# Gated cross attention on one core: the next quad's scores behind the last attention block, two transposes issued earlier, one sum in another buffer

## The chip, the cores and the metric

The kernel runs on one core of one Trainium2 chip. The metric is the device time of one execution in microseconds (us). Lower is better. The five engines of a core have queues of their own and run in parallel: PE (matrix products), DVE and POOL (elementwise work), ACT (activations and copies), and SP, which issues most of the transfers. [...] In profile lines PEld is the loading of weights into the PE array.

## What is computed

Eight sequences of 1024 rows (x, width 1024) attend to eight short memories (64 rows, width 512). Everything is float32.

```python
memory_proj = jnp.einsum('bme,de->bmd', memory, W_mem)
scores = jnp.einsum('bnd,bmd->bnm', hidden_states, memory_proj) / jnp.sqrt(jnp.float32(D))
attn = jax.nn.softmax(scores, axis=-1)
memory_context = jnp.einsum('bnm,bmd->bnd', attn, memory_proj)
gate_input = jnp.concatenate([hidden_states, memory_context], axis=-1)
gate = jax.nn.sigmoid(jnp.einsum('bnf,df->bnd', gate_input, W_gate) + b_gate)
fused = hidden_states + gate * memory_context
return _rmsnorm(fused, norm_w)
```

The large product is x (8192 x 1024) times the upper half of W_gate (1024 x 1024). The lower half is applied to the memory once (`mg`), so that attention needs only two products with 64 memory rows each: one gives the context, one its share of the gate.

## The kernel before, in words

**Quads.** The 8192 rows are cut into 16 quads of 512 rows, q = 0 to 15, two to a sequence. A quad's x is transposed into four tiles, a11, a12, a21 and a22 (`A[q, r, half]`), by eight instructions `transpose_x` on DVE: two for each tile.

**Products and slots.** The product with W_gate is done in Strassen-Winograd form at two levels. One quad has seven outer products, in the order 1, 6, 7, 5, 4, 2, 3 (`ORDER`, L527), and each has seven inner products A, B, C, D, A', E, F: A' adds onto A. One inner product is one slot, so a quad has 49 (`SLOTS`), slot 0 being A of outer product 1. In a slot PE issues two matmuls in the source, which are four records in the profile. In what follows C(5) is inner product C of outer product 5. In the profile all elementwise sums come from line 95 and all matmuls from line 92, so instructions are told apart by the names of their tiles.

**The sums around them.** These come with each outer product:

- `outer_s` (DVE) forms left operands of whole products. Those of a quad are S1 and S2 (for products 5 and 6), S3 = a11 - a21, written over a21 (for product 7), and S4 = a12 - S2 (for product 3).
- `inner_s(q, o, part)` (POOL) forms the left operands s1 to s4 of the inner products of o: part 0 gives s1 and s2, part 1 gives s3 and s4. They are put on the list one outer product ahead, at its slots 1 and 5, and are shown as tile `l`. B reads s2, C reads s3, D reads s1, F reads s4.
- u2, u3 and u4 (DVE) take B, C and D out of PSUM, each on top of the one before; ACT copies A first.
- `pre` (POOL) adds u3, u3 and u4 into output tiles, `fin` (DVE) adds A, D, E and F.
- `norm`, `gated` (DVE), `sigmoid`, `square` (ACT) and `residual` (a transfer from POOL's queue that adds x) finish a quad's output, partly during the next quad.

**The order.** Every engine runs its instructions in the order of the program (`pin`). That order is written by hand: `at(slot, ...)` puts work ahead of the matmuls of a slot, `mid((q, o), ...)` puts it behind the attention products of outer product o of quad q and ahead of its `fin` sums. Inside a slot the order is that of registration.

**Attention.** The last four outer products (5, 4, 2, 3) each hold a block of 16 matmuls between A' and E, two at a time: each uses 64 of the 128 rows of the array (`64*128` in the profile). They accumulate into A, F, E and D as well as into two tiles `pc`. `scores(q)` (L295) is 32 records in the profile on all rows and 64 columns (`128*64`), again two at a time, and a copy to `sT` on ACT; it reads all four tiles of x of its quad, k = 0 to 3 from a11 and a21 and the rest from a12 and a22. It stands ahead of slot 7, so between outer products 1 and 6. `transpose_scores` follows at slot 9, the softmax at slots 10 and 13, `transpose_attn` (tile `pa`) at slot 18.

**PSUM.** Five banks rotate over the tiles A to F. F shares B's bank. The next outer product's A, B, C, D and E take the banks of this one's C, D, A, E and F.

**Ahead of the loop.** The memory is projected (`pm`), its projection is spread over four tiles m11 to m22 (`mpT`), and `mg` is made by seven products with sums of the lower weights (`mg_product`). Their order is 1, 6, 5, 2, 7, 4, 3, and `mp_step` makes three sums for them. The third, s3 = m11 - m21 on POOL (L463), is read by product 7, the fifth of the seven. It lies in the rotating buffers `l2`, of which there are two; later tenants of the same pair are c21 and, in turn, the operands of `inner_s`. POOL's queue behind s3 reads: four inner sums of weight block 7, one sum for `mg`, `inner_s(0, 1, ...)` for the first quad, and twelve inner sums of the weight blocks 5, 6 and 4.

Of the kernel before, what the change touches and what calls it, by code (L numbers as in the profile page):

```python
# [10 lines left out]
ALU = mybir.AluOpType  # L11
# [9 lines left out]
def tile_gated_cross_attention_rmsnorm(  # L21
# [42 lines left out]
    nc = tc.nc  # L64
# [18 lines left out]
    rot = ctx.enter_context(tc.tile_pool(name="rot", bufs=2))  # L83
    small = ctx.enter_context(tc.tile_pool(name="small", bufs=1))
# [9 lines left out]
    def tt(eng, o, a, b, op):  # L94
        pin(eng.tensor_tensor(o, a, b, op))  # L95
# [4 lines left out]
    def t4k(pool, shape, tag, name):  # L100
        return pool.tile(shape, F32, tag=tag, name=name)
# [33 lines left out]
    for k in range(KD):  # L135
        t = t4k(*((gpool, [P, D], "gate") if k < 7 else (apool, [P, D], "s4")), f"w2_{k}")
# [28 lines left out]
    def w1_place(o):  # L165

        if o in (5, 6, 4):
            outer_b[o] = const.tile([P, 4, H], F32, tag=f"t{o}", name=f"t{o}")
        inner_t[o] = const.tile([P, 3, 2, C], F32, tag=f"it{o}", name=f"it{o}")
# [237 lines left out]
    def mp_step(eng, tag, pool, a, b, op):  # L407
        t = t4k(pool, [P, KH, HM], tag, f"mp_{tag}")
        tt(eng, t, a, b, op)
        return t  # L410
# [49 lines left out]
    s2 = mp_step(nc.vector, "s2", apool, s1, m11, ALU.subtract)  # L460
    outer_sum(7, 3, 7)
    w1_place(7)
    s3 = mp_step(nc.gpsimd, "l2", rot, m11, m21, ALU.subtract)  # L463
    for n in range(4):
        inner_sum(nc.gpsimd, 7, n)
    c11 = mg_tile(rot, "u", "mg_c11")
# [53 lines left out]
    def at(slot, fn, *args):  # L520
        due.setdefault(slot, []).append(lambda: fn(*args))

    def mid(key, fn, *args):
        beside.setdefault(key, []).append(lambda: fn(*args))
# [5 lines left out]
    def plan(q):  # L530
        t0 = SLOTS * q
        nxt = q + 1 < NQ
        order = [o for o, _ in ORDER]
        for i, o in enumerate(order):
            for part, t in ((0, 1), (1, 5)):
                if i + 1 < len(order):
                    at(t0 + 7 * i + t, inner_s, q, order[i + 1], part)
                elif nxt:
                    at(t0 + 7 * i + t, inner_s, q + 1, order[0], part)
        at(t0 + 7, scores, q)  # L540
        at(t0 + 7, outer_s, q, 3)
        at(t0 + 7, outer_s, q, 4)
        at(t0 + 9, transpose_scores, q)
        at(t0 + 10, softmax_a, q)
        at(t0 + 13, softmax_b, q)
        at(t0 + 18, transpose_attn, q)
        at(t0 + 21, attn_difference, q)
        if not nxt:
            at(t0 + 5, load_last)
            return  # L550
        at(t0 + 2, load_xq, q + 1)
        for t in (2, 3):
            mid((q, 5), transpose_x, q + 1, t, 0)
            mid((q, 2), transpose_x, q + 1, t, 1)
        for i, t, half in ((36, 0, 0), (38, 1, 0), (43, 0, 1), (45, 1, 1)):
            at(t0 + i, transpose_x, q + 1, t, half)
        mid((q, 3), outer_s, q + 1, 1)
        mid((q, 3), outer_s, q + 1, 2)
        if (q + 1) % QPB == 0:
            at(t0 + 10, load_mp, (q + 1) // QPB)  # L560
            at(t0 + 49, load_mg, (q + 1) // QPB)
        if q % QPB == 0:
            at(t0 + 8, add_bias, q // QPB)
# [249 lines left out]
    for q in range(NQ):  # L813
        plan(q)
        for o, ext in ORDER:
            outer_product(q, o, ext)
# [29 lines left out]
```

## Time and profile before

| what | us |
|---|---|
| three runs | 982.54, 982.60, 982.59 |
| their median | 982.59 |
| the profiled execution's own time | 982.54 |
| its span, first to last instruction | 980.7 |
| one quad in the middle, A(1) to the next A(1) | 55.05 |
| first A(1) of the loop, after the start of the span | 83.98 |

The span is what the views divide up; 1.84 us of the execution's own time lie outside it. Of the span PE is busy for 98%, DVE for 84%, POOL for 74% and ACT for 33%. TensorE's granted clock is 0.996 on average. Quads 1 to 14 repeat each other: four of them, measured from A(1) to A(1), took 55.04, 55.05, 55.05 and 55.05 us. One slot without a wait takes 0.864 us.

A line of the timeline gives the start, the time taken, the engine, the source line, the operation, the tiles it writes and reads with their sizes, and in brackets how long the engine had been idle and for whom it waited. A matmul's line with "x4" covers the four records of a slot, and its end is modelled; starts are what to compare.

### The profile page before, as it was taken

How to read it: one execution, taken by the hardware profiler on the slowest of the kernel's cores; microseconds unless marked ns; L12 is line 12 of the kernel's file. 1: busy time of each engine (PE TensorE's matmuls, PEld its weight loads, DVE VectorE, ACT ScalarE, POOL GpSimd, SP SyncE). 2: the span in 40 equal slices, each digit the busy share in tenths (PEclk: the TensorE clock that was granted, in tenths of full speed). 3: DMA queues.
4: the chain of work that ended last, by engine and by line, in shares of the span. 5: the costliest groups of instructions: out<-in, count | busy, mean ns of one | idle time of the engine just before them, and what ended most of it. 6: DMA issues, size and time to landing. Idle time of an engine off the chain costs nothing.

```text
span 980.7 us, 14277 instructions
## 1 busy us (share of the span) xinstructions
PE 965.9 (98%) x4938; PEld 770.1 (79%) x4938; DVE 819.0 (84%) x1487; ACT 324.9 (33%) x602; POOL 730.5 (74%) x881
## 2 busy tenths in 40 slices
PE   9999999999999999999999999999999999999995
PEld 7546788888888888888887888888887888888873
DVE  3877788979797988979797988979797988979787
ACT  1100234152333334161433334151433334151434
POOL 3329977878787887878787877878787877878772
PEclk9999999999999999999999999999999999999998
DMA  9865264381918364382918374482918374482612
GB/s 374 258 157 141 35 110 117 91 200 55 192 65 156 113 137 112 97 194 58 189 65 160 109 139 110 100 190 62 185 65 163 111 139 104 106 185 66 170 65 86
DMA packets 71255, 128.32 MB, mean 131 GB/s; under 512 B 12432, under 2 KB 49296, under 8 KB 70928
## 3 DMA queue, kind: packets, MB, share of 16 engines
q1 hardware_dynamic: 61760, 93.34, 35.3%
q0 software_dynamic: 9280, 33.56, 18.5%
q8 instruction: 39, 0.64, 0.3%
q10 hardware_dynamic: 144, 0.52, 0.2%
q14 instruction: 32, 0.26, 0.1%
HBM read 87.56 MB, written 39.85 MB: 130 GB/s over the span
## 4 chain that ended last, share of the span: by engine, by line
PE 93%; POOL 3%; DVE 2%; issue 1%; ACT 0%; DVEq 0%; POOLq 0%; ACTq 0%
PE kA L92 19%; PE pc L92 12%; PE kE L92 11%; PE kF L92 10%; PE kD L92 10%; PE kC L92 9%; PE kB L92 9%; PE psT L92 6%; PE pg L92 4%; PE pm L92 3%; POOL it L95 1%; DVE gate L95 1%; POOL l L95 1%; POOL gate L95 1%; PE pz L92 0%
## 5 line engine op out<-in xcount | busy, mean ns | idle before, releaser
L95 POOL TENSOR_TENSOR gate<-gate,u 128x256 f32<-128x256 f32 x336 | 270.4, 835 | 115.8 <-DVE u L95 110.1
L582 ACT ACTIVATE gate<-gate 128x512 f32<-128x512 f32 x128 | 79.0, 629 | 400.3 <-DVE gate L95 400.3
L95 POOL TENSOR_TENSOR l<-a 128x256 f32<-128x256 f32 x128 | 128.4, 1003 | 74.1 <-DVE a L95 55.8
L248 DVE STREAM_TRANSPOSE a<-xq 128x512 f32<-128x512 f32 x128 | 138.1, 1101 | 4.0 <-DMA mgd<-mpq 4.0
L92 PE MATMUL pc<-mg,attnT 64*128 64x256 f32 x512 | 127.4, 389 | 0.0
L611 DVE SCALAR_TENSOR_TENSOR gate<-gate,ss,nw_sb 128x512 f32<-128x512 f32 x120 | 126.0, 1059 | 1.1
L92 PE MATMUL kB<-it,l 128*128 128x256 f32 x448 | 115.1, 379 | 0.0
L92 PE MATMUL kD<-it,l 128*128 128x256 f32 x448 | 115.0, 379 | 0.0
L92 PEld LDWEIGHTS pc<-mg,attnT 64*128 64x128 f32 x512 | 90.6, 186 | 29.7 <-issue 21.2
L92 PE MATMUL kA<-w,a 128*128 128x256 f32 x384 | 98.7, 379 | 0.4 <-ACT u L726 0.4
L92 PEld LDWEIGHTS kB<-it,l 128*128 128x128 f32 x448 | 85.0, 190 | 11.9 <-DVE gate L95 0.4
L92 PEld LDWEIGHTS kD<-it,l 128*128 128x128 f32 x448 | 85.1, 190 | 11.6
L95 DVE TENSOR_TENSOR gate<-gate,pc 128x512 f32<-128x512 f32 x128 | 87.2, 681 | 5.8 <-ACT gate L582 5.8
L92 PEld LDWEIGHTS kA<-w,a 128*128 128x128 f32 x384 | 71.6, 190 | 10.2 <-ACT u L726 0.8
L95 POOL TENSOR_TENSOR l<-s 128x256 f32<-128x256 f32 x96 | 76.6, 797 | 1.6 <-PE kF L92 1.5
L726 ACT COPY u<-kA 128x256 f32<-128x256 f32 x112 | 40.5, 362 | 101.8 <-PE kA L92 99.7
L92 PE MATMUL kE<-it,a 128*128 128x256 f32 x256 | 69.0, 392 | 0.0
L95 DVE TENSOR_TENSOR u<-u,kB 128x256 f32<-128x256 f32 x112 | 45.5, 407 | 27.6 <-PE kB L92 24.9
L92 PE MATMUL kA<-t,s 128*128 128x256 f32 x256 | 67.4, 386 | 0.0
L92 PE MATMUL kC<-w,l 128*128 128x256 f32 x256 | 65.8, 379 | 1.4 <-POOL l L95 1.4
L92 PE MATMUL kF<-w,l 128*128 128x256 f32 x256 | 65.7, 379 | 0.0
L596 ACT ACTIVATE junk<-gate 128x1024 f32<-128x1024 f32 x60 | 63.5, 1058 | 1.9 <-DMA gate<-in_x 1.0
(123 smaller groups left out, 1996.4 us busy)
## 6 DMA issues: line engine op xcount, KB each, us to landing
xq<-in_x SPq DMA_DIRECT2D x64, 512.0 KB, 9.5
gate<-in_x POOLq DMA_DIRECT2D x60, 512.0 KB, 7.9
out<-gate SPq DMA_DIRECT2D x60, 512.0 KB, 2.6
w<-in_w_gate_t SPq DMA_DIRECT2D x8, 512.0 KB, 11.0
w<-in_w_gate_t SPq DMA_DIRECT2D x2, 2048.0 KB, 15.6
mg<-mgd SPq DMA_DIRECT2D x16, 256.0 KB, 3.8
mpd<-mpT SPq DMA_DIRECT2D x4, 512.0 KB, 3.7
mgd<-mpq SPq DMA_DIRECT2D x16, 128.0 KB, 2.7
```

The lines of the kernel that those rows point to most:

```text
L92: pin(nc.tensor.matmul(o, lhsT, rhs, start=start, stop=stop, skip_group_check=True))
L95: pin(eng.tensor_tensor(o, a, b, op))
L248: nc.vector.transpose(A[key][:, :, r * P : (r + 1) * P], chunks(xq[q][:, 4 * t : 4 * t + 4, :], KD)[:, half * KH : (half + 1) * KH],)
L582: pin(nc.scalar.activation(g, g, AF.Sigmoid))
L596: nc.scalar.activation(junk, O[q, t], AF.Square, accum_out=ss[:, t % 2 : t % 2 + 1])
L611: nc.vector.scalar_tensor_tensor(g[:, cols], g[:, cols], rstd[:, t % 2 : t % 2 + 1], nw_sb[:, cols], ALU.mult, ALU.mult,)
L726: pin(nc.scalar.copy(p1, kb["A"]))
```

## The change

The change has three edits.

1. `s3` of the memory's sums moves from the two rotating buffers `l2` to the single buffer `junk` of the pool `small`. Its earlier tenant is the block of zeros that warms up PE at the start; its next are the `square` results of quad 0, which come after its last outer product.
2. `scores(q)` stays ahead of slot 7 for quad 0 alone. The other quads' scores are issued one quad sooner, in `mid((q, 3), ...)`: right behind the attention products of outer product 3 of the quad before, ahead of E(3), and ahead of the two sums `outer_s(q + 1, 1)` and `(q + 1, 2)`.
3. The two transposes that finish a12 of the next quad move from slots 43 and 45 to slots 42 and 43, so that they are ahead of u2 and u3 of outer product 3.

```diff
@@ -460,7 +460,7 @@
     outer_sum(7, 3, 7)
     w1_place(7)
-    s3 = mp_step(nc.gpsimd, "l2", rot, m11, m21, ALU.subtract)
+    s3 = mp_step(nc.gpsimd, "junk", small, m11, m21, ALU.subtract)
     for n in range(4):
         inner_sum(nc.gpsimd, 7, n)
@@ -537,7 +537,8 @@
-        at(t0 + 7, scores, q)
+        if q == 0:
+            at(t0 + 7, scores, q)
         at(t0 + 7, outer_s, q, 3)
         at(t0 + 7, outer_s, q, 4)
@@ -552,8 +553,9 @@
-        for i, t, half in ((36, 0, 0), (38, 1, 0), (43, 0, 1), (45, 1, 1)):
+        for i, t, half in ((36, 0, 0), (38, 1, 0), (42, 0, 1), (43, 1, 1)):
             at(t0 + i, transpose_x, q + 1, t, half)
+        mid((q, 3), scores, q + 1)
         mid((q, 3), outer_s, q + 1, 1)
         mid((q, 3), outer_s, q + 1, 2)
```

## The prediction

> **What bounds the kernel now.** I read the granted clock first (0.996, nothing to explain there), then the busy times, then the waits of PE.
>
> ```profile
> PE 965.9 (98%) x4938; PEld 770.1 (79%) x4938; DVE 819.0 (84%) x1487; ACT 324.9 (33%) x602; POOL 730.5 (74%) x881
> ```
>
> ```profile
> POOL l L95 <- PE pg L92: 18.3, 1, 18.3
> ...
> PE kC L92 <- POOL l L95: 1.4, 1, 1.4
> ```
>
> The columns of a wait are the sum, how often, and the longest. PE is the bound, and hardly waits for an operand: once, 1.4 us, in the first quad, and three times, 1.6 us together, in the last. So time is won only by giving PE less to do or by removing that one wait, and is lost wherever PE is made to wait. The upper line is POOL's one long wait, ahead of the loop. The timeline of the first quad shows where it comes out:
>
> ```profile
> 100.09 1.03 PE L92 MATMUL kA<-w,a 128*128 128x256 f32 x4
> 101.11 1.13 PE L92 MATMUL kB<-it,l 128*128 128x256 f32 x4
> 103.60 1.13 PE L92 MATMUL kC<-w,l 128*128 128x256 f32 x4 [1.37 <-POOL l L95]
> 104.57 1.03 PE L92 MATMUL kD<-it,l 128*128 128x256 f32 x4
> ```
>
> A slot is 0.864 us, so D(7) was due at 100.09 + 3 x 0.864 = 102.68 and starts at 104.57: 1.89 us lost. POOL came late with s3 because its queue had stood still.
>
> Then the timeline of a quad in the middle, q = 8, with A(1) at 581.29, all engines, from F(1) to C(5):
>
> ```profile
> 586.47 1.03 PE L92 MATMUL kF<-w,l 128*128 128x256 f32 x4
> 587.43 3.67 PE L92 MATMUL psT<-a,mpb 128*64 128x256 f32 x32
> 587.53 0.42 DVE L95 TENSOR_TENSOR gate<-u,kF 128x256 f32<-128x256 f32 x1 [0.44 <-PE kF L92]
> 589.42 1.22 DVE L95 TENSOR_TENSOR a<-a,a 128x1024 f32<-128x1024 f32 x1 [1.47 <-PE psT L92]
> 590.57 1.22 DVE L95 TENSOR_TENSOR s<-a,s 128x1024 f32<-128x1024 f32 x1
> 590.73 1.64 POOL L95 TENSOR_TENSOR l<-a 128x256 f32<-128x256 f32 x1 [3.71 <-DVE a L95]
> 591.03 1.13 PE L92 MATMUL kA<-t,s 128*128 128x256 f32 x4
> 593.13 0.42 DVE L95 TENSOR_TENSOR u<-u,kB 128x256 f32<-128x256 f32 x1 [1.35 <-PE kB L92]
> ...
> 601.80 0.42 DVE L95 TENSOR_TENSOR u<-u,kC 128x256 f32<-128x256 f32 x1
> 602.36 2.10 POOL L95 TENSOR_TENSOR gate<-gate,u 128x256 f32<-128x256 f32 x3 [1.54 <-DVE u L95]
> 604.41 0.73 POOL L95 TENSOR_TENSOR l<-s 128x256 f32<-128x256 f32 x1
> 605.19 0.82 PEld L92 LDWEIGHTS kC<-t,l 128*128 128x128 f32 x4
> 605.39 0.81 PE L92 MATMUL kC<-t,l 128*128 128x256 f32 x3
> ```
>
> The reader is to see two things. During the scores (3.6 us) DVE and POOL catch up: DVE idles 1.47 and 1.35 us, POOL 3.71. From u2(6) at 593.13 to u3(7) at 601.80 no DVE line has an idle time in brackets. And at the end s3 for C(5) is ready at 604.41 + 0.73 = 605.14, with its weights loading from 605.19: the margin is about nothing. The scores at slot 7 are the breathing space that makes this chain just fit.
>
> **What the Trainium skill says.** "TensorEngine Tiling (Array Packing)", section Key Properties: changing the tiling mode, not just the tile, drains the array. The trace agrees: around the scores, 591.03 to 592.00 (B) and 586.47 to 587.43 are 0.97 and 0.96 where a slot is 0.864, and 587.43 to 591.03 is 3.60 for 16 pairs of 0.216 (3.456): 0.35 us for two switches. Around attention in outer product 5, A' at 607.12, E at 610.00, F at 610.97 give 3.85 less two slots and 8 pairs: 0.39. "SBUF — State Buffer", section Who interferes with whom: a DVE instruction with two SBUF inputs contends with a GpSimd instruction that reads SBUF. The trace agrees: POOL's s1 takes 1.64 beside S4, against a median of 0.73. "TensorE: Matmul & The Clock Gate", section Step-by-step: weights are loaded ahead of the running matmul. Here the load leads by 0.20; after a late operand that lead is gone (C and D of 103.60 and 104.57 are 0.97 apart, 0.10 extra).
>
> **Part 1, the switches.** Before, one quad has four switches for its scores and its last attention block, 0.35 + 0.39 = 0.74. After, the array goes from full to rows, rows to columns, columns to full: three. The direct switch between the two tilings isn't in this trace. Bounds: free (saves 0.37), or as dear as both it replaces (saves nothing). I take one average switch, 0.74 / 4 = 0.185, and so a saving of 0.185. It is on PE, which is the bound, in 15 quads: **-2.8 us** (0 to -5.5). The matmuls themselves and the ACT copy only move; no transfer moves with them. ACT waits over 7 us there for the next sigmoid, so the 0.37 us copy is hidden.
>
> **Part 2, what loses its cover.** All times here are us after A(1) of a quad. From B(6) on, PE runs earlier by 0.96 + 3.60 + 0.97 - 2 x 0.864 = 3.80. C(5), before at 24.10, would be due at 20.30.
>
> DVE: `fin` of F(1) starts at 6.24, as before, since F(1) does not move. Then S3 follows at once, with no scores to wait for; the wait that is late next is DVE's own queue. 0.34 to S3, 1.15 from S3 to S4, 1.15 from S4 to u2(6) (the same size of instruction), the packed 8.67 from u2(6) to u3(7), 0.42 for that: u3(7) is done at 17.97, before at 20.93. So DVE gains 2.96 where PE gains 3.80.
>
> POOL: the two sums for product 7 start with S3 and are done by about 10.7, so they don't matter. `pre` of product 7 waits for u3(7): 0.14 to start, 2.05 until s3 starts, 0.73 for s3, 0.05 to the load: 20.94. PE waits from 20.30 to 20.94 and loses 0.10 for the lead: 0.74. Smaller waits ahead of it are inside this one, not added: B(7) for the bank that `fin` of D(6) frees (0.1), `pa` for the softmax (0.2). Once PE has waited, the distances behind are again those of before, so it does not wait a second time in the quad; and since A(1) to F(1) of the next quad has slack (DVE idles 0.97 ahead of `fin` of E(1)), the same wait comes again in each of the quads 1 to 15.
>
> In the seven even quads from 2 on, POOL also has `add_bias` ahead of the `pre` of product 6 (0.83 us in quad 2, which was hidden in 1.7 us of waiting). Now it pushes s3(7) to about 14.4 to 14.8 where C(7) is due at 14.04: 0.5 to 0.95 with the lead, in place of 0.74. I take 0.85. Sum: 8 x 0.74 + 7 x 0.85 = **+11.9 us**. Bounds: 0.6 a quad if the lead costs nothing, 1.05 if a `norm` (0.75 alone, 1.05 beside POOL) is held up 0.3 by the second sum for product 7, which now falls on it: +9 to +15.8.
>
> **Part 3, the transposes.** Each takes 1.04 to the next start. u2 and u3 of product 3 move back by 1.04, u4 not. `gated` of product 2, between them, then ends at 632.42 instead of 631.38, and attention overwrites its tile at about 632.58: it just fits. 0, at most 0.1 a quad. POOL's `pre` of product 3 starts 1.04 later, hidden by the scores ahead of E(3).
>
> **Part 4, s3's buffer.** With it `inner_s(0, 1)` no longer waits for product 7 of `mg` at 70.4; next it waits for the transposes of a11, at 56.7, and the inner sums for DVE's `outer_sum` of 6 and 4 (62.0 and 68.9). POOL's list of twelve then ends near 78, not 91.2. In quad 2, whose POOL wasn't behind, s3(7) had 1.0 us to spare, and quad 0 keeps its scores at slot 7. So the 1.89 goes: **-1.9 us**. Against it: POOL now runs beside DVE's sums of b21 (64.2 to 66.7), which PE needs at 70.25; stretching them as other sums were stretched (0.69 to 1.4) uses 2.8 of these 3.6 us. Bounds -1.9 to -0.9.
>
> **The sum** against the execution's own 982.54 (span 980.7, 1.84 outside it; the median of the runs is 0.05 higher): 982.54 - 2.8 + 11.9 - 1.9 = 989.7.
>
> **The rivals.**
> - *No wait appears.* PE keeps its distance and the two gains stand: 982.54 - 2.8 - 1.9 = 977.8. For it: PE is the only bound on the page, and DVE and POOL idle 16% and 26%. Against it: that idle time isn't between F(1) and C(5). It decides from 0.31 us a quad (4.7 / 15): the chain from F(1) to s3(5) would have to be 0.43 shorter than summed. Chance 0.19.
> - *It balances:* about 0.3 us a quad, 982.5. Chance 0.06.
> - *POOL and DVE hold each other up:* the upper bound plus 0.1 a quad for `gated`: 982.54 + 17.3 - 2.8 - 1.9 = 995.1. For it, norms beside POOL took 1.05 to 1.24. Chance 0.13.
> - My forecast: 0.62. With its costs' bounds, its own range is 985 to 995.
>
> **Chances.** About 0.2% (2 us) can be told from no change. Slower 0.62 + 0.13 = 0.75, same 0.06, faster 0.19. The range goes from 979 to 996: below it lies the first rival but for its weaker forms (0.15 left out), above it the third's worst third (0.04).
>
> **What would show it.** Right: new waits of kC on POOL's `l` in product 5 (and in even quads in product 7), some 0.7 us each; a quad of about 55.6; DVE without idle time from `fin` of F(1) to u3(7); in quad 0 no wait at C(7). Wrong: quads of 54.9 without waits (then the chain was shorter), or a direct switch that costs more than 0.35.

## The result, and the profile after

| | before | after |
|---|---|---|
| median of four runs, us | 982.60 | 1022.66 |
| lowest and highest | 982.54, 982.68 | 1021.59, 1024.38 |
| the profiled execution's own time; its span | 982.54; 980.7 | 1021.59; 1019.8 |
| one odd quad in the middle, A(1) to A(1) | 55.05 | 55.64 |
| one even quad in the middle | 55.05 | 60.37 |
| mean granted clock | 0.996 | 0.986 |

The change makes the kernel slower by 4%: ratio 1.041, interval 1.0394 to 1.0425. The direction was forecast, the size was not: 989.7 was expected, and 33 us more came. The table already says where to look. Odd quads are what was predicted (55.6); the even ones, from quad 4 to quad 14, lose another 4.7 us each, and quad 2 another 3.0.

The page's first part and the list of waits of the kernel after (sum, how often, longest; PEld is the weight load, PE the product):

```profile
PE 979.6 (96%) x4938; PEld 775.8 (76%) x4938; DVE 843.5 (83%) x1487; ACT 327.2 (32%) x602; POOL 728.7 (71%) x881
```

```profile
PEld kB L92 <- DVE gate L95: 31.2, 15, 4.1
...
PEld kC L92 <- POOL l L95: 3.9, 8, 0.5
...
PE kB L92 <- DVE gate L95: 25.1, 7, 3.7
```

The busy shares hardly tell the two kernels apart: PE still shows 96%. The waits do. PE waits seven times, once per even quad from 2 on, for 25.1 us together. The eight waits of kC on POOL's `l` are the odd quads' and are the predicted ones. In the chain of work that ended last PE's share falls from 93% to 77%, and DVE has 13% of it.

**An odd quad.** Timeline of the kernel after, quad 9, whose A(1) is at 605.45, from `fin` of F(1) to D(5):

```profile
611.69 0.42 DVE L95 TENSOR_TENSOR gate<-u,kF 128x256 f32<-128x256 f32 x1 [0.44 <-PE kF L92]
612.03 1.22 DVE L95 TENSOR_TENSOR a<-a,a 128x1024 f32<-128x1024 f32 x1
613.16 1.22 DVE L95 TENSOR_TENSOR s<-a,s 128x1024 f32<-128x1024 f32 x1
614.30 0.41 DVE L95 TENSOR_TENSOR u<-u,kB 128x256 f32<-128x256 f32 x1
...
623.03 0.42 DVE L95 TENSOR_TENSOR u<-u,kC 128x256 f32<-128x256 f32 x1
623.59 2.10 POOL L95 TENSOR_TENSOR gate<-gate,u 128x256 f32<-128x256 f32 x3 [1.53 <-DVE u L95]
625.64 0.73 POOL L95 TENSOR_TENSOR l<-s 128x256 f32<-128x256 f32 x1
626.42 1.13 PE L92 MATMUL kC<-t,l 128*128 128x256 f32 x4
627.39 1.03 PE L92 MATMUL kD<-it,l 128*128 128x256 f32 x4
```

This is the predicted chain, link by link: F(1)'s sum, S3 at once, S4, u2(6) at 8.85 after A(1) (8.87 was summed), a packed DVE queue to u3(7), `pre`, s3, and C(5) at 20.97 (20.94). D follows C after 0.97, so the lead of the load is lost as expected.

**An even quad.** Quad 8, whose A(1) is at 545.08, from u3(6), which `pre` of product 6 reads, to B(7):

```profile
555.12 0.41 DVE L95 TENSOR_TENSOR u<-u,kC 128x256 f32<-128x256 f32 x1
...
555.73 0.83 POOL L372 DMA_DIRECT2D mg<-in_b_gate  x1
...
556.31 2.37 POOL L95 TENSOR_TENSOR gate<-gate,u 128x256 f32<-128x256 f32 x3
...
556.57 4.70 DVE L613 SCALAR_TENSOR_TENSOR gate<-gate,ss,nw_sb 128x512 f32<-128x512 f32 x1
...
558.37 0.99 POOL L95 TENSOR_TENSOR l<-a 128x256 f32<-128x256 f32 x1
...
559.05 0.98 POOL L95 TENSOR_TENSOR l<-a,l 128x256 f32<-128x256 f32 x1
559.73 0.97 POOL L95 TENSOR_TENSOR l<-s 128x256 f32<-128x256 f32 x1
560.78 1.07 POOL L95 TENSOR_TENSOR l<-l,s 128x256 f32<-128x256 f32 x1
...
561.52 0.41 DVE L95 TENSOR_TENSOR gate<-gate,kD 128x256 f32<-128x256 f32 x1
...
561.98 1.98 PE L92 MATMUL kB<-it,l 128*128 128x256 f32 x4 [3.57 <-DVE gate L95]
```

The reader is to see the norm at 556.57. It is one half of a `norm`, the same 128 x 512 instruction that takes 0.74 alone and 1.06 beside POOL. Here it takes 4.70. It stands ahead of the `fin` sums of product 6, and B(7) needs the bank that `fin` of D(6) frees: DVE is through with that at 561.93 and B(7) starts at 561.98. A(7) was at 557.38, so B(7) was due at 558.24 and is 3.74 late.

POOL meanwhile works off `add_bias` and seven sums with hardly a pause. They start 0.68 us apart (558.37, 559.05, 559.73), until s2 of product 5, which reads the s1 made just before it: 1.05 from 559.73 to 560.78 where the same pair takes 0.80 elsewhere. The norm ends in that step, at 561.27. All seven even quads show the same: one norm each of 4.68 to 4.81, and none over 1.6 elsewhere.

**The clock behind the wait.** The table by stage of the same quad (window, us, busy time and count of PE, PEld, DVE, ACT, POOL; then granted clock, DMA share, GB/s). The windows run from A(7) to B(7), B to C, C to D, and D to the transpose `pa` behind it:

```profile
557.38:561.98 4.60, 1.03 (x5) 0.57 (x4) 4.60 (x4) 1.27 (x2) 4.39 (x6) 1.00 0.63 124
561.98:563.75 1.77, 1.77 (x4) 1.42 (x5) 1.70 (x5) 1.72 (x5) 0.00 (x0) 0.54 0.73 296
563.75:565.46 1.71, 1.71 (x6) 1.35 (x4) 1.49 (x4) 1.26 (x2) 0.00 (x0) 0.50 0.00 0
565.46:566.36 0.90, 0.90 (x5) 0.75 (x4) 0.42 (x1) 0.00 (x0) 0.11 (x1) 0.97 0.65 264
```

After 3.57 us without a product PE is granted half its clock for two slots: 1.77 and 1.71 in place of 0.864, so 1.75 us more. That and the 3.74 make 5.49; the quad measures 60.37 against 54.87 (55.05 less the 0.185 of the switches), 5.50.

The slow clock does not follow every time. In quad 2 the same norm takes 4.68 and B(7) comes as late, 4.59 behind A(7), but the granted clock stays at 1.00 behind it and the next slots take 0.96 and 0.87. That quad takes 58.68. Against odd quads of 55.64 the seven even ones (58.68 and six of 60.36 to 60.49) lose 31.5 together in the profiled execution. So its 39 us (1021.59 less 982.54) divide, with the experiments' numbers below, into -1.6 for the buffer, +8.9 for the moved scores in fifteen quads, and +31.5 for the norm of the even quads: 38.8 by this sum. It is the fastest of the four executions; by the medians the difference is 40.1.

### The profile page after: what moved, and what is told of

Its sections match the earlier page's. It is cut to its first block, busy times and chain, and to the rows that moved or that the text cites. A ratio compares the mean times of both kernels' runs of the same rounds, so it can differ in the third digit from the quotient of the medians.

```text
span 1019.8 us, 14307 instructions
## 1 busy us (share of the span) xinstructions
PE 979.6 (96%) x4938; PEld 775.8 (76%) x4938; DVE 843.5 (83%) x1487; ACT 327.2 (32%) x602; POOL 728.7 (71%) x881
## 4 chain that ended last, share of the span: by engine, by line
PE 77%; DVE 13%; issue 6%; POOL 3%; DMA 1%; ACT 0%; DVEq 0%; POOLq 0%; ACTq 0%
PE kA L92 13%; PE pc L92 11%; PE kE L92 9%; PE kC L92 8%; PE kF L92 7%; PE kD L92 7%; PE kB L92 7%; PE psT L92 6%; PE pg L92 5%; DVE gate L95 3%; DVE gate L613 3%; PE pm L92 3%; DVE u L95 2%; POOL gate L95 2%; DVE a L95 2%
## 5 line engine op out<-in xcount | busy, mean ns | idle before, releaser
L95 POOL TENSOR_TENSOR gate<-gate,u 128x256 f32<-128x256 f32 x336 | 283.8, 886 | 139.6 <-DVE u L95 135.5
L92 PE MATMUL kB<-it,l 128*128 128x256 f32 x448 | 121.6, 396 | 25.2 <-DVE gate L95 25.1
L613 DVE SCALAR_TENSOR_TENSOR gate<-gate,ss,nw_sb 128x512 f32<-128x512 f32 x120 | 144.3, 1212 | 1.1
L95 POOL TENSOR_TENSOR l<-a 128x256 f32<-128x256 f32 x128 | 115.1, 899 | 39.3 <-PE kB L92 34.8
L95 DVE TENSOR_TENSOR gate<-gate,kE 128x256 f32<-128x256 f32 x112 | 45.5, 418 | 50.5 <-PE kE L92 45.6
L92 PE MATMUL kC<-w,l 128*128 128x256 f32 x256 | 70.9, 402 | 0.0
L95 DVE TENSOR_TENSOR gate<-gate,kF 128x256 f32<-128x256 f32 x112 | 45.6, 419 | 27.4 <-PE kF L92 23.0
```

The costliest lines, as they stand in the source:

```text
L92: pin(nc.tensor.matmul(o, lhsT, rhs, start=start, stop=stop, skip_group_check=True))
L613: nc.vector.scalar_tensor_tensor(g[:, cols], g[:, cols], rstd[:, t % 2 : t % 2 + 1], nw_sb[:, cols], ALU.mult, ALU.mult,)
```

## The experiments

### The buffer alone

The kernel before with edit 1 and nothing else. `e1_buffer_only`, as a diff to the kernel after:

```diff
-        if q == 0:
-            at(t0 + 7, scores, q)
+        at(t0 + 7, scores, q)
...
-        for i, t, half in ((36, 0, 0), (38, 1, 0), (42, 0, 1), (43, 1, 1)):
+        for i, t, half in ((36, 0, 0), (38, 1, 0), (43, 0, 1), (45, 1, 1)):
...
-        mid((q, 3), scores, q + 1)
```

> The kernel before with edit 1 alone (s3 in the other buffer). If the wait in quad 0 is worth what the changed kernel's trace shows there (1.89 us lost before, about 0.3 after), the time is 981.0 (980.7 to 981.3), with no waits of PE from quad 1 on. If the early inner sums cost DVE more than they free, it is 982.6 or above.

Measured: 980.74 against 982.35, ratio 0.9984 (0.9977 to 0.999), so -1.6 us. The timeline of quad 0, from C(7):

```profile
101.60 1.03 PE L92 MATMUL kC<-w,l 128*128 128x256 f32 x4
102.47 1.03 PE L92 MATMUL kD<-it,l 128*128 128x256 f32 x4
103.63 0.41 PE L342 MATMUL pa<-ident,e 128*128 128x128 f32 x2
103.87 1.03 PE L92 MATMUL kA<-w,a 128*128 128x256 f32 x4
```

C(7) follows B(7) without a wait. From D(7) to `pa` it is 1.16, though, 0.3 more than a slot: the softmax, until now hidden by the wait at C(7), is late next. That is the difference between the 1.9 predicted and the 1.6 found.

### Is it the moved scores, or `add_bias` with them?

What sets even quads apart is `add_bias`, a transfer from POOL's queue at slot 8, between the sums of product 6 and `pre`. `e2_bias_slot6` is the kernel after with that transfer two slots sooner, where POOL waits for S3 anyway:

```diff
         if q % QPB == 0:
-            at(t0 + 8, add_bias, q // QPB)
+            at(t0 + 6 if q else t0 + 8, add_bias, q // QPB)
```

> The changed kernel with add_bias at slot 6 in place of slot 8 (quads 2, 4, ... 14), so that POOL issues it while it waits for S3. Theory A (the 4.7 us norm comes from what add_bias does to POOL's queue directly ahead of pre of product 6): no norm over 1.3 us, all quads at about 55.6, 989.6 in total (988.5 to 991). Rival (the long norm belongs to even quads for another reason, such as the transfers of x, mg or out at that place): still 4.7 us and near 1022.

Measured: 989.68 against 982.35, ratio 1.0074 (1.0059 to 1.0089). Quads 1 to 14 take 55.58 to 55.65, no norm is over 1.32, and its waits are those of an odd quad, fifteen times:

```profile
PEld kC L92 <- POOL l L95: 7.3, 15, 0.5
PEld kB L92 <- DVE gate L95: 6.3, 15, 0.4
```

So one transfer, at this place, costs 33 us of the 40. Moving the scores costs 989.68 - 980.74 = 8.9 us over the buffer alone, 0.6 a quad, close to the predicted net of 0.74 lost and 0.185 gained.

Of the same two edits, the transposes are told apart by `f3_old_transposes`, which is `e2_bias_slot6` with edit 3 undone:

```diff
-        for i, t, half in ((36, 0, 0), (38, 1, 0), (42, 0, 1), (43, 1, 1)):
+        for i, t, half in ((36, 0, 0), (38, 1, 0), (43, 0, 1), (45, 1, 1)):
```

> The kernel with add_bias at slot 6 (989.7), but with the two transposes back at slots 43 and 45: edits 1 and 2 without edit 3. If edit 3 is worth nothing, as I costed it: 989.7 within 0.5. If the scores need it (they would wait for the last transpose), 0.5 us a quad or more: 997 or above.

Measured: 989.57, ratio 1.0072 (1.0057 to 1.0087), the same. Edit 3 is worth nothing that can be told here.

### What keeps the norm waiting?

In the kernel before the same transfer stood ahead of the same `pre`, with the same norm beside it, and nothing happened. Its timeline in quad 8:

```profile
538.07 0.83 POOL L372 DMA_DIRECT2D mg<-in_b_gate  x1
...
538.62 0.75 DVE L611 SCALAR_TENSOR_TENSOR gate<-gate,ss,nw_sb 128x512 f32<-128x512 f32 x1
...
539.29 0.42 DVE L95 TENSOR_TENSOR u<-u,kC 128x256 f32<-128x256 f32 x1
...
539.84 2.55 POOL L95 TENSOR_TENSOR gate<-gate,u 128x256 f32<-128x256 f32 x3 [0.95 <-issue]
...
540.74 1.06 DVE L611 SCALAR_TENSOR_TENSOR gate<-gate,ss,nw_sb 128x512 f32<-128x512 f32 x1
```

There POOL pauses 0.95 between the transfer and its sums. The profile names no releaser for it, but `pre` reads u3(6), which ends at 539.71, and `pre` starts 0.13 later. In quad 14, where the transfer is issued later, the releaser is named: 0.43 for DVE's `u`. After the change u3(6) ends at 555.53, before the transfer is issued at 555.73, so nothing is left to pause for: this is how moving the scores closed the gap. Two things are to be separated: the transfer, and the pause behind it.

The expectations below call "the shared port" the access to SBUF over which DVE and POOL would hold each other up, and "descriptor writing" what POOL would do to issue a transfer; both are suppositions there. The four kernels of this part add work and ran once each, so what is read from them is above all the norm in their traces.

**Something else in the transfer's place.** `e3_filler` is `e2_bias_slot6` with one more sum on POOL, over 208 columns, at the transfer's old place. It takes 0.62 us, as long as the load of the next kernel; `add_bias` takes 0.83. The sum stands in every quad from 1 on.

```diff
+    filler = t4k(small, [P, 208], "filler", "filler")
+
+    def fill():
+        tt(nc.gpsimd, filler, nw_sb[:, 0:208], nw_sb[:, 208:416], ALU.add)
...
+        if q:
+            at(t0 + 8, fill)
```

> As the kernel with add_bias at slot 6, and in each quad from 1 on a POOL sum of two slices of 208 columns into a spare tile at slot 8, where add_bias stood; it adds work and no transfer. Theory A1 (POOL, once late, runs from one ready instruction to the next, and the norm of DVE finds no gap at the shared port): long norms of 4 to 5 us in all 15 quads, some 60.4 us each, 1060 in total. Theory A2 (the descriptor writing of the transfer holds the port): no norm over 1.4 us; POOL is only 0.6 us later, 990 to 999.

Measured: 993.6, and no norm over 1.36. Its timeline shows the same position as in the kernel after, with the norm 0.24 to 0.26 behind the start of `pre` in both:

```profile
545.00 0.62 POOL L95 TENSOR_TENSOR filler<-nw_sb 128x208 f32<-128x208 f32 x1
...
545.58 2.55 POOL L95 TENSOR_TENSOR gate<-gate,u 128x256 f32<-128x256 f32 x3
545.82 1.04 DVE L620 SCALAR_TENSOR_TENSOR gate<-gate,ss,nw_sb 128x512 f32<-128x512 f32 x1
```

So theory A1 fails: a POOL queue that is merely full, or a norm that merely meets `pre` at this moment, is not the cause. It takes the transfer.

**Another transfer in its place.** `f2_plain_load` has, instead of that sum, a plain load from POOL's queue: 208 columns of norm_w, into a tile that nobody reads. `add_bias` stays at slot 6.

```diff
+    def fill():
+        pin(nc.gpsimd.dma_start(filler, norm_w[0:208].partition_broadcast(P)))
...
+        if q:
+            at(t0 + 8, fill)
```

> As the kernel with add_bias at slot 6, and in each quad from 1 on a plain load from POOL's queue (norm_w, 208 columns to 128 partitions of a spare tile, no accumulation) at slot 8; it adds work. Theory C1 (any transfer that POOL issues in that place does it): norms of 4 to 5 us in all 15 quads, 1055 to 1065. Theory C2 (it takes add_bias, its accumulation or its 256 KB): no norm over 1.6 us, 989 to 996.

Measured: 1073.58, above the range given, but with one norm of 4.46 to 4.48 in each of the fifteen quads, as theory C1 says. Quads 3 to 14 take 61.43 to 61.45, quads 1 and 2 take 60.15. The picture is that of the even quads:

```profile
580.83 0.62 POOL L239 DMA_DIRECT2D filler<-in_norm_w  x1
...
581.46 2.09 POOL L95 TENSOR_TENSOR gate<-gate,u 128x256 f32<-128x256 f32 x3
...
581.66 4.48 DVE L620 SCALAR_TENSOR_TENSOR gate<-gate,ss,nw_sb 128x512 f32<-128x512 f32 x1
...
586.85 2.08 PE L92 MATMUL kB<-it,l 128*128 128x256 f32 x4 [3.36 <-DVE gate L95]
```

So it does not take what `add_bias` does with its data: a small load does the same. The excess over the range is the clock. In most quads it stays low for longer than in the kernel after (three slots of 1.87, 1.71 and 1.70 in the quad shown; mean 0.952), though PE's wait is shorter (3.36); in quad 1 it is two slots, 1.84 and 1.68.

**A pause behind the transfer.** `f1_gap_after_bias` is the kernel after with four memsets on POOL behind `add_bias` in even quads. They only write. The sums follow 1.5 us later.

```diff
+    def fill():
+        for _ in range(4):
+            pin(nc.gpsimd.memset(filler, 0.0))
...
             at(t0 + 8, add_bias, q // QPB)
+            if q:
+                at(t0 + 8, fill)
```

> The changed kernel, add_bias at slot 8 as there, and directly behind it in the even quads four fills of a spare tile by POOL, which write SBUF and read nothing; they add work. Theory B1 (the norm is kept out by POOL's reading sums that follow the transfer without a gap): during the fills the norm gets through, no norm over 1.6 us, even quads within 1.5 us of 55.6, 989 to 1001 in total. Theory B2 (the transfer's descriptor writing alone keeps it out): norms of 4 to 5 us stay, 1020 or more.

Measured: 999.34, and no norm over 1.30:

```profile
546.89 0.83 POOL L378 DMA_DIRECT2D mg<-in_b_gate  x1
...
547.44 1.55 POOL L240 MEMSET filler<- 128x208 f32 x4
...
547.73 0.74 DVE L621 SCALAR_TENSOR_TENSOR gate<-gate,ss,nw_sb 128x512 f32<-128x512 f32 x1
...
548.96 2.54 POOL L95 TENSOR_TENSOR gate<-gate,u 128x256 f32<-128x256 f32 x3
```

Adding work to POOL took 23 us away, and theory B2 fails. The norm that began behind the transfer and beside writes alone ran at its own 0.74. What is left over `e2_bias_slot6`, 9.7 us, is POOL's delay: in even quads PE now waits 0.62 for B(7) and 0.91 for C(7).

**A dependent pair.** In the kernel after the norm ended where one POOL sum needed the result of the one just before. `g1_dependent_pair` puts such a pair directly behind `add_bias`: two sums that read, and no pause by idling or by writes.

```diff
+    def fill():
+        tt(nc.gpsimd, filler, nw_sb[:, 0:208], nw_sb[:, 208:416], ALU.add)
+        tt(nc.gpsimd, filler, filler, nw_sb[:, 208:416], ALU.add)
...
             at(t0 + 8, add_bias, q // QPB)
+            if q:
+                at(t0 + 8, fill)
```

> The changed kernel, add_bias at slot 8 as there, and directly behind it in the even quads two POOL sums of 208 columns, both reading SBUF, the second reading what the first wrote; they add work. In the traces the long norm ended where POOL came to such a pair (s2 on s1). Theory D1 (the wait of a dependent POOL sum on the one before is gap enough for the norm): no norm over 1.6 us, 994 to 1001. Theory D2 (it takes a longer stretch without reads, like the fills): norms of 4 us and more stay, 1022 or more.

Measured: 1001.67, 0.7 above the range given, and no norm over 1.33:

```profile
547.96 0.83 POOL L378 DMA_DIRECT2D mg<-in_b_gate  x1
...
548.53 0.91 POOL L95 TENSOR_TENSOR filler<-nw_sb 128x208 f32<-128x208 f32 x1
...
548.79 1.21 DVE L621 SCALAR_TENSOR_TENSOR gate<-gate,ss,nw_sb 128x512 f32<-128x512 f32 x1
...
549.52 0.96 POOL L95 TENSOR_TENSOR filler<-filler,nw_sb 128x208 f32<-128x208 f32 x1
```

From the first sum of the pair to the second it is 0.99 here, against 0.58 from such a sum to the next in `e3_filler`. The norm ends at 550.00, 0.48 behind the start of the second sum; in the kernel after it ended 0.49 behind the start of s2 (561.27 and 560.78). This fits theory D1: the norm is served where POOL first has to wait for itself.

Taken together: a transfer from POOL's queue with POOL's sums directly behind it keeps DVE's norm, which reads two inputs from SBUF, waiting until POOL first has to pause. "SBUF — State Buffer", section Who interferes with whom, of the Trainium skill says that such a DVE instruction contends with a GpSimd instruction that reads SBUF, not with one that only writes it. The runs agree (4.70 beside sums behind the transfer, 0.74 beside the memsets behind it). The section also says, of another case (DVE's two-port modes), that whoever issues first has the shared ports for the whole instruction. Taken over to this one, that would hold the norm for one of POOL's instructions; it was held over seven. Why a transfer ahead of the stream turns one instruction into seven was not tried and stays open.

### Giving the chain its time back

The chain account says that F(1) to C(5) is 0.74 too long because S3 and S4 stand in it, 1.15 each. The last three kernels take them out.

`g2_s3_early_only` is `e2_bias_slot6` with S3 alone moved to the place behind S1 and S2, during the attention of product 3. `e4_sums_early` is the kernel after with S3 there and S4 at slot 5, `add_bias` staying at slot 8. `f4_sums_early_bias6` is `e4_sums_early` with `add_bias` at slot 6. The edit of `e4_sums_early`:

```diff
-        at(t0 + 7, outer_s, q, 3)
-        at(t0 + 7, outer_s, q, 4)
+        if q == 0:
+            at(t0 + 7, outer_s, q, 3)
+        at(t0 + 5 if q else t0 + 7, outer_s, q, 4)
...
         mid((q, 3), outer_s, q + 1, 2)
+        mid((q, 3), outer_s, q + 1, 3)
```

> The changed kernel with S3 of the next quad behind S1 and S2 in the mid of outer product 3, and S4 at slot 5 in place of slot 7 (quads 1 on); add_bias stays at slot 8. My account of the 0.77 us (DVE's queue from fin of F(1) to u3(7) is packed and 0.84 too long): taking 2.3 us out of it frees the chain, no waits of PE in quads 1 to 14, quads of 54.87, 978.3 (977.8 to 979.5). If the chain is not DVE's queue but POOL's, it stays at 55.6 a quad in odd quads, 989 or more.

> The kernel with add_bias at slot 6 (989.7), with S3 alone moved into the mid of outer product 3; S4 stays at slot 7. By my account the packed chain of DVE was 0.77 us too long a quad, and this takes 1.15 us out of it: no waits of PE from the chain, 978 to 980. If S4, or POOL, holds the chain as well, half of the gain or less: 984 or more.

> The kernel with S3 and S4 early, and add_bias at slot 6 as well. My account says add_bias is harmless wherever POOL has a gap behind it, as it has there already: 978.9 within 0.5. If what is left of waits in that kernel comes from add_bias, 977 to 978.

| kernel | us | before beside it | ratio (interval) |
|---|---|---|---|
| `e4_sums_early` | 978.87 | 982.35 | 0.9964 (0.9951 to 0.9977) |
| `g2_s3_early_only` | 978.91 | 982.33 | 0.9964 (0.995 to 0.9978) |
| `f4_sums_early_bias6` | 978.80 | 982.47 | 0.9961 (0.9947 to 0.9975) |

All three beat both kernels, and don't differ from each other by more than these runs can tell. One sum out of the chain is enough, as its account says: 1.15 out, 0.74 too long. Of quads 1 to 14 of `e4_sums_early` ten take 54.84 or 54.85, as expected. Four even ones (4, 8, 10 and 14) take 54.90 to 55.10, with small waits in products 5 and 4; in the other two kernels single even quads take up to 55.54. These waits, mostly for POOL's sums and ACT's copies, were not followed up. Quad 8 of `e4_sums_early`, an even one, from u2(6) to C(5):

```profile
535.07 0.42 DVE L95 TENSOR_TENSOR u<-u,kB 128x256 f32<-128x256 f32 x1 [0.66 <-PE kB L92]
...
544.28 2.10 POOL L95 TENSOR_TENSOR gate<-gate,u 128x256 f32<-128x256 f32 x3 [1.54 <-DVE u L95]
546.35 0.72 POOL L95 TENSOR_TENSOR l<-s 128x256 f32<-128x256 f32 x1
...
547.33 1.03 PE L92 MATMUL kC<-t,l 128*128 128x256 f32 x4
```

DVE waits for PE again ahead of u2(6), 0.66, and s3 is ready at 547.07, 0.26 ahead of C(5). With `add_bias` at slot 8 POOL has 0.91 us of idle time behind it in this kernel, and the norm takes 1.05: the pause is back, and with it the harmless form. `g2_s3_early_only` and `f4_sums_early_bias6`, with `add_bias` at slot 6, don't depend on that pause, which makes them the sounder ones, though they are no faster.

## Why the size was wrong

- **Part 1, the switches, held.** Three switches in place of four, with a direct one from rows to columns. In quad 8 of the kernel after, A'(3) is at 597.13, the scores at 600.01, E(3) at 603.62, F(3) at 604.59. That is 7.46 less two slots, 8 pairs and 16 pairs of 0.216: 0.55 for three switches. 0.74 less 0.55 is 0.19, taken as 0.185. Quads without a wait say the same: 55.05 less 54.85 is 0.20. In total `e4_sums_early` gains 1.9 over the buffer alone, not 2.8, because some of its even quads wait.
- **Part 2, odd quads, held.** 0.74 predicted; 0.77 lost, though not at one place: (quad 9) 0.19 at B(7), 0.10 in the slot behind it, 0.14 at `pa` and 0.35 at C(5) and in the slot behind it. That B(7) and `pa` were "inside this one, not added" is borne out by C(5), which comes when it was summed to come.
- **Part 2, even quads, failed.** The step is "Now it pushes s3(7) to about 14.4 to 14.8 [...] I take 0.85". It charges `add_bias` with one thing, 0.83 us of POOL's time. It leaves out that a norm could be kept waiting behind the transfer. The runs put 5.5 there: 3.74 at B(7), where the norm holds up the bank, and 1.75 of slow clock; C(7), where the wait was expected, has none of its own, nor has C(5). The term was 7 x 0.85 = 6. In the profiled execution it measured 36.9 (3.8 in quad 2, 5.5 to 5.6 in the other six), and the difference of 30.9 is nearly the whole error of the forecast there, 31.9. (By the prediction's own figures the upper end of its range is 14.8 - 14.04 + 0.10 = 0.86, not 0.95, which changes nothing.)
- **Why the bound did not catch it.** The upper bound allowed a norm "held up 0.3", taken from norms that met POOL in the kernel before. In that trace `add_bias` has a pause of 0.94 to 0.95 behind it in quads 2 to 12 and of 0.43 in quad 14, and the packed sums that norms met have no transfer directly ahead of them. The bound was right for both and said nothing of the two together, which only the change brings about. The quad of the prediction's long timeline, with A(1) at 581.29, is quad 9 and not 8: an odd one, without the transfer.
- **The third rival** had the right pair, norm and POOL in each other's way, but not the transfer, and priced it like the bound: 995.1.
- **Part 3 held** (`f3_old_transposes`). **Part 4** came to 1.6, not 1.9: the softmax's `pa`, not named in that part of the prediction, keeps 0.3. POOL's list of twelve ends at 81.3 in the kernel after, not near 78; it was early enough all the same.
- Of the signs listed, the quad of 55.6, DVE without idle time up to u3(7), the waits of kC in product 5 (smaller than said, since part of the loss falls ahead of them) and quad 0's C(7) came true; the waits of kC in product 7 of even quads did not.

## What to carry to other kernels

When an edit removes an engine's breathing space, list what will then run back to back that never did before, instructions that issue transfers above all: a duration measured with a pause in between is no bound for it. A long wait of PE is to be priced with the slow clock that can come behind it: in the kernel after, waits of 3.6 us cost half as much again in six of seven quads. And before scores or any other block of PE work is moved away, its cover should be paid for first: one DVE sum of 1.15 us moved elsewhere turned +8.9 us into about -1.8 on top of the buffer's gain.

## What the runs showed of the hardware that was not expected

- A norm with two inputs from SBUF took 4.68 to 4.81 us in place of 1.06 to 1.14 in all seven even quads, and 4.46 to 4.48 behind a plain 208-column load in `f2_plain_load`. A sum as long as that load in its place gave 1.04, a pause of writes behind it 0.74, a dependent pair 1.21.
- PE's clock after a wait: 0.54 and 0.50 for about 3.5 us after 3.57 without a product (quad 8 of the kernel after). "TensorE: Matmul & The Clock Gate", section Why this matters for your kernels, of the Trainium skill advises against idle gaps of PE of more than about 3 us for this reason. The trace agrees in six of the seven even quads; in quad 2 a gap of 3.56 left the clock at 1.00. In `f2_plain_load` gaps of about 3.35 were followed by a slow stretch in all fifteen quads, of differing length. After the waits of 0.6 to 1.2 us in `f1_gap_after_bias` and `g1_dependent_pair` the mean clock stayed at 0.996.
